# Attention values of head 0 scaled on VectorE instead of ScalarE

## The chip, the core and the metric

The kernel runs on one core of a Trainium2 chip. The metric is device time in microseconds, of which the median of three runs is given. One further execution was taken by the hardware profiler; its times are those of the views below. The engines are TensorE (PE, with its weight loads as PEld), VectorE (DVE), ScalarE (ACT), GpSimd (POOL) and SyncE (SP). [...]

## What is computed

A transformer block in three parts: half a mixture-of-experts layer, attention, and a second half mixture-of-experts layer. Attention has 4 batches of 512 rows with 256 features, and 3 heads. Cut to what matters here:

```
Q = einsum('bne,hde->hbnd', x, Wq); K = ... Wk; V = ... Wv
scores = einsum('hbnd,hbmd->hbnm', Q, K) * scale
w = softmax(scores, axis=2)
attn = einsum('hbnm,hbmd->hbnd', w, V)
out = mean(attn, axis=0) @ fc_w.T + fc_b
```

The softmax runs over axis 2, the query axis `n`, so that the sum that divides belongs to a row `m` of the values. It can therefore be multiplied into the values instead of the scores.

## The kernel before

The block is one long program for one core. The first expert layer, attention for the four batches `b`, and the second expert layer follow each other; the second layer's norm, router and row scatters of a batch are issued inside the attention of the next one. The order of instructions on each engine is made by a scheduler from the program text, the dependencies and some hand-set order constraints; each engine then runs its list in order.

For each batch and head `h`, four steps matter:

- `query(h)` (from L863) multiplies the normed, transposed input `xnT` by the folded weights `A[h]` into the tile `py` (L868). ScalarE copies it to `y` (L872).
- `quadrants(h)` (from L874) forms the 512 x 512 scores in `ex` with seven half-size products (`product(i, ...)`, tile `psc`, L896), as in Strassen's scheme. VectorE combines them (L911, L914, L915, L917, L918, L920), ScalarE copies two (L910, L912) and GpSimd adds one (L913). `exps` then takes the maximum of two slices on VectorE (L903, one reduction over 1024 elements a row) and the exponential on ScalarE (L905), which also yields the sums `z`. L922 makes `rz = 1/z`. `exps(2)` is issued between L918 and L920, `exps(0)` after L920.
- `value(h)` (from L924) computes for each of four slices `m` the product `pv` of `xnT` and `G[h]` (L929; `G` folds the value weights and the output layer), and evicts it from PSUM to `v`, scaled by `rz`. Before the change, head 1 is evicted by VectorE (L934), heads 0 and 2 by ScalarE (L938).
- The loop at the end sums `pa = ex^T v` over heads and slices (L970) and adds it to `x` (L975).

All three heads' scores come first, then all three heads' values. Hence the evictions of head 0 stand next to the score combination and the exponentials of head 2.

PSUM has eight banks here: three in a ring named `mm`, three in a ring named `dn`, and one each for the router's tiles. `py`, `pv`, `pa` and the score products with even numbers use `mm`. The odd-numbered score products use `dn`, as do the transposes `pt_lna` and `pt_ln` of the layernorms (L284). A new tile of a ring can be written once the tile three places earlier has been read out. By the program's text the ring `dn` goes `psc` 7, 5, 3 of head 2, then `pt_lna` (two tiles), then `pt_ln` (two tiles). Product 5 is read by L917 and L918, product 3 by L920.

The transposes belong to the layernorm of the next batch (`lna`) and to that of the second expert layer for the batch before (`ln`). Their results are copied out by ScalarE (L288) and VectorE (L292), and the router's score products `psr` (L335) and rank products `psk` (L400) follow.

Of the kernel before, what the change touches and what calls it, by code (L numbers as in the profile page):

```python
# [21 lines left out]
def tile_macaron_block(  # L22
# [35 lines left out]
    NH = Wq.shape[0]  # L58
# [785 lines left out]
    for b in range(B):  # L844
# [79 lines left out]
        def value(h):  # L924
            v = vs[h] = att.tile([P, NJ, H], F32, tag="y", name=f"v_{b}_{h}", bufs=4)
            for m in range(NJ):
                pv = psum.tile([P, H], F32, tag="mm", name=f"pv_{b}_{h}_{m}")
                for c in range(NC):
                    nc.tensor.matmul(  # L929
                        pv, xnT[:, c, m * P : (m + 1) * P], G[h][:, c, :],  # L930
                        start=(c == 0), stop=(c == NC - 1),
                    )
                if h == 1:
                    nc.vector.tensor_scalar(  # L934
                        v[:, m, :], pv, rzs[h][:, m : m + 1], None, ALU.mult
                    )
                else:
                    nc.scalar.mul(v[:, m, :], pv, rzs[h][:, m : m + 1])  # L938
# [12 lines left out]
        for h in range(NH):  # L951
            value(h)
# [126 lines left out]
```

## Time and profile before

| | us |
|---|---|
| median of 3 runs | 538.14 |
| lowest and highest | 537.95, 538.39 |
| the profiled execution | 540.54 |
| its span | 538.7 |

| group | count | busy us | mean ns |
|---|---|---|---|
| ACT v<-pv,rz (L938) | 32 | 14.7 | 469 |
| DVE v<-pv,rz (L934) | 16 | 7.3 | 480 |
| DVE nmax<-ex (L903), 188 to 400 us | 21 | 25.5 | 1214 |

How to read the views. A row of a timeline gives start and length in us, engine, line, operation, written tile <- read tiles, shapes and the number of merged instructions; in square brackets stands the idle time before it and what ended that. Consecutive starts lie closer together than the lengths, because instructions overlap at their ends. A row of the waits names the waiting engine and line, the line that it waited for, the total in us, how many times, and the longest. Float32 matrix products show as two records for each product.

### The profile page before, as it was taken

The numbers are of one execution on the slowest core, as the hardware profiler recorded it, in microseconds if no ns is written. First come the engines' busy times: TensorE is split into PE (matmuls) and PEld (weight loads), VectorE is DVE, ScalarE is ACT, GpSimd is POOL, SyncE is SP. The second block draws the span as 40 slices with busy tenths as digits, with TensorE's granted clock in tenths as the row PEclk, the third lists the DMA queues.
The fourth block names the chain that finished last, engine by engine and source line by source line (L and its number), as shares of the span: only waits on it lengthen the run. The fifth ranks groups of instructions, "written<-read, shape, count | busy, mean of one in ns | idle before, by whom it ended". The sixth has DMA issues, their size and how long they took to land. (4 is left out here: it accounts for less than half of the span.)

```text
span 538.7 us, 7948 instructions
## 1 busy us (share of the span) xinstructions
PE 484.5 (90%) x2262; PEld 374.9 (70%) x2262; DVE 295.4 (55%) x981; ACT 224.6 (42%) x514; POOL 234.7 (44%) x281
## 2 busy tenths in 40 slices
PE   8977249999999899999999999999999767999984
PEld 4666037888656788678885778867888445788852
DVE  6834345555787771258325883336753642555565
ACT  3743015666543770255402664054630313466630
POOL 2466714665658321242254512553014174355653
PEclk9877769999999999999999999999999886999998
DMA  7993364557420000000012000200002245255856
GB/s 266 357 370 125 118 226 122 164 161 230 170 89 1 2 0 1 0 0 2 2 69 89 0 2 0 79 2 1 1 11 99 64 171 178 90 165 179 273 177 208
DMA packets 34734, 57.39 MB, mean 107 GB/s; under 512 B 4928, under 2 KB 25408, under 8 KB 34688
## 3 DMA queue, kind: packets, MB, share of 16 engines
q1 hardware_dynamic: 25424, 32.99, 19.7%
q0 software_dynamic: 8160, 23.44, 12.0%
q10 hardware_dynamic: 1104, 0.42, 0.3%
q8 instruction: 20, 0.33, 0.3%
q14 instruction: 26, 0.21, 0.1%
HBM read 30.78 MB, written 26.05 MB: 105 GB/s over the span
## 5 line engine op out<-in xcount | busy, mean ns | idle before, releaser
L671 POOL DMA_INDIRECT y_d<-ey,to x82 | 80.0, 976 | 66.5 <-ACT xt L632 45.8
L438 POOL DMA_INDIRECT xn_d<-xn_ln,pos x64 | 62.5, 977 | 91.7 <-DVE fa L489 23.0
L644 PE MATMUL peg<-gu,xt 128*128 x328 | 87.5, 391 | 1.9 <-DVE g L597 1.6
L970 PE MATMUL pa<-v,ex 128*128 128x256 f32 x384 | 86.2, 382 | 0.0
L970 PEld LDWEIGHTS pa<-v,ex 128*128 128x128 f32 x384 | 71.6, 190 | 9.2
L644 PEld LDWEIGHTS peg<-gu,xt 128*128 128x128 f32 x328 | 57.6, 195 | 9.0 <-issue 1.7
L661 DVE COPY hT<-pht 128x128 f32<-128x128 f32 x82 | 23.8, 291 | 60.1 <-issue 28.6
L666 PE MATMUL pey<-dn,hT 128*128 x164 | 50.4, 390 | 5.6 <-DVE hT L661 4.6
L670 ACT ACTIVATE ey<-pey,xg 128x256 f32<-128x256 f32 x82 | 38.9, 474 | 28.0 <-issue 15.7
L929 PE MATMUL pv<-G,xnT_lna 128*128 128x256 f32 x192 | 43.5, 382 | 2.7 <-ACT v L938 2.1
L868 PE MATMUL py<-xnT_lna,A 128*128 128x512 f32 x96 | 42.7, 593 | 1.0 <-DVEq L710 1.0
L929 PEld LDWEIGHTS pv<-G,xnT_lna 128*128 128x128 f32 x192 | 36.0, 190 | 9.6 <-ACT v L938 3.3
L905 ACT ACTIVATE ex<-ex,nmax 128x512 f32<-128x512 f32 x48 | 34.2, 714 | 18.6 <-DVE nmax L903 18.4
L650 ACT ACTIVATE sig<-peg 128x128 f32<-128x128 f32 x82 | 22.8, 278 | 42.7 <-PE peg L644 27.3
L632 ACT COPY xt<-pxt 128x256 f32<-128x256 f32 x82 | 29.8, 366 | 14.6 <-PE pxt L628 8.4
L605 PE MATMUL po<-sd,h 128*128 128x256 f32 x64 | 17.1, 415 | 19.1 <-DVE h L598 17.7
L975 DVE TENSOR_TENSOR x<-x,pa 128x256 f32<-128x256 f32 x16 | 6.7, 420 | 50.1 <-PE pa L970 41.3
L666 PEld LDWEIGHTS pey<-dn,hT 128*128 128x128 f32 x164 | 25.2, 194 | 12.4 <-issue 5.1
L628 PE MATMUL pxt<-ident,xg 128*128 128x128 f32 x164 | 32.3, 279 | 0.9 <-DVE xnT_ln L292 0.8
L872 ACT COPY y<-py 128x512 f32<-128x512 f32 x24 | 13.8, 581 | 46.1 <-PE py L868 46.0
L868 PEld LDWEIGHTS py<-xnT_lna,A 128*128 128x128 f32 x96 | 18.2, 190 | 20.6 <-issue 19.8
L881 POOL TENSOR_TENSOR right<-y 128x256 f32<-128x256 f32 x12 | 9.3, 775 | 50.0 <-ACT y L872 50.0
(201 smaller groups left out, 876.0 us busy)
## 6 DMA issues: line engine op xcount, KB each, us to landing
xg<-xn_d SPq DMA_DIRECT2D x82, 129.0 KB
gu<-ffn_experts_gate_up_dram SPq DMA_DIRECT2D x4, 1024.0 KB
yg<-y_d SPq DMA_DIRECT2D x8, 512.0 KB
y<-y_d SPq DMA_DIRECT2D x6, 512.0 KB
dn<-_L_ffn_experts_down_dram SPq DMA_DIRECT2D x2, 1024.0 KB
x<-in_L_attn_x_dram SPq DMA_DIRECT2D x3, 512.0 KB
out_dram<-x SPq DMA_DIRECT2D x3, 512.0 KB
y_d<-ey,to POOLq DMA_INDIRECT x82
```

What stands on the lines that cost most here:

```text
L438: ins = nc.gpsimd.indirect_dma_start(out=self.xn_v[k * NT + b * NJ + j], out_offset=bass.IndirectOffsetOnAxis(ap=pos[:, k, j : j + 1], axi ...
L628: ins = nc.tensor.transpose(pt[:, c, :], xg[:, c * P : (c + 1) * P], ident)
L632: nc.scalar.copy(xt, pt)
L644: nc.tensor.matmul(pg, xt[:, c, :], gu[:, bass.ds(e, 1), c, :], start=(c == 0), stop=(c == NC - 1),)
L661: self.flips.append(nc.vector.tensor_copy(hT, pt))
L666: self.downed = nc.tensor.matmul(py, hT, dn[:, bass.ds(e, 1), :], start=True, stop=True)
L670: nc.scalar.mul(y, py, xg[:, H + 1 : W])
L671: ins = nc.gpsimd.indirect_dma_start(out=self.y_v[i], out_offset=bass.IndirectOffsetOnAxis(ap=tos[i], axis=0), in_=y, in_offset=None,)
L868: nc.tensor.matmul(py, A[h][:, c, fc * P : (fc + 1) * P], xnT[:, c, :], start=(c == 0), stop=(c == NC - 1),)
L905: nc.scalar.activation(ex[:, m, :], ex[:, m, :], AF.Exp, bias=nmax[:, m : m + 1], accum_out=z[:, m : m + 1],)
L929: nc.tensor.matmul(pv, xnT[:, c, m * P : (m + 1) * P], G[h][:, c, :], start=(c == 0), stop=(c == NC - 1),)
L970: nc.tensor.matmul(pa, es[h][:, m, j * P : (j + 1) * P], vs[h][:, m, :], start=(h == 0 and m == 0), stop=(h == NH - 1 and m == NJ - 1),)
```

## The change

The condition that chooses the engine of an eviction in `value(h)` is widened. `NH` is 3.

```diff
-                if h == 1:
+                if h < NH - 1:
                     nc.vector.tensor_scalar(
                         v[:, m, :], pv, rzs[h][:, m : m + 1], None, ALU.mult
                     )
                 else:
                     nc.scalar.mul(v[:, m, :], pv, rzs[h][:, m : m + 1])
```

The four evictions of head 0 in each batch, 16 in all, are issued on VectorE. Head 1 stays there and head 2 stays on ScalarE. The numbers computed are the same. Since the scheduler places the instructions anew, others move too. On TensorE the transposes (L284), which stood behind all twelve value tiles of a batch, stand after the fourth (batch 0) or the third (batches 1 to 3). In batches 1 and 2 the two halves of `pt_ln` stand on either side of the fourth value tile, and one product of the router's eight is issued before the fifth. ScalarE's copies of the transposed tiles (L288) stand between the two pairs of exponentials of head 2. VectorE's copy (L292) stands ahead of the reciprocal L922 of head 2, and in batches 1 and 2 a second one between the evictions of head 1.

## The prediction

> **What bounds the kernel now.** I read the page's engine shares first, then the waits of TensorE between 186 and 400 us (the four attention batches), then the timelines of TensorE, VectorE and ScalarE around the value products of each batch.
>
> ```profile
> PE 484.5 (90%) x2262; PEld 374.9 (70%) x2262; DVE 295.4 (55%) x981; ACT 224.6 (42%) x514; POOL 234.7 (44%) x281
> L929 PE MATMUL pv<-G,xnT_lna 128*128 128x256 f32 x192 | 43.5, 382 | 2.7 <-ACT v L938 2.1
> ```
>
> TensorE is the busiest engine and the start of the chain that ended last. Its waits in the attention part are short and all but one belong to the value products (L929):
>
> ```profile
> PE pv L929 <- ACT v L938: 2.1, 3, 0.8
> PE py L868 <- DVEq L710: 1.0, 1, 1.0
> PE pv L929 <- DVE ex L915: 0.7, 2, 0.4
> ```
>
> So the most that better placed evictions can win is small, and whatever new wait TensorE gets between 186 and 416 us is paid nearly in full: the only other wait there, at the branch L710, hangs on VectorE's last add of pa (L975), which follows TensorE. Here is batch 1: TensorE, then VectorE, then ScalarE (start, length, engine, line, operation):
>
> ```profile
> 249.40 5.34 PE L929 MATMUL pv<-G,xnT_lna 128*128 128x256 f32 x24
> 255.39 5.45 PE L929 MATMUL pv<-G,xnT_lna 128*128 128x256 f32 x24 [0.65 <-ACT v L938]
> ```
>
> ```profile
> 251.64 0.66 DVE L918 TENSOR_TENSOR ex<-ex,psc 128x512 f32<-128x512 f32 x1
> 252.21 1.21 DVE L903 TENSOR_REDUCE nmax<-ex 128x2 f32<-128x1024 f32 x1
> 253.34 0.68 DVE L920 TENSOR_TENSOR ex<-ex,psc 128x512 f32<-128x512 f32 x1
> 254.05 1.22 DVE L903 TENSOR_REDUCE nmax<-ex 128x2 f32<-128x1024 f32 x1
> 255.19 0.87 DVE L934 TENSOR_SCALAR v<-pv,rz 128x256 f32<-128x256 f32 x2
> ```
>
> ```profile
> 254.18 0.71 ACT L905 ACTIVATE ex<-ex,nmax 128x512 f32<-128x512 f32 x1
> ...
> 254.88 0.45 ACT L938 ACTIVATE v<-pv,rz 128x256 f32<-128x256 f32 x1
> ```
>
> Each value tile is 4 records (192 over 48 tiles). Records start every (5.34 - 0.38) / 23 = 0.216 us, so a tile is 0.863 us. I write V h.m for head h, slice m. All value tiles share three PSUM banks, so each waits for the eviction of the tile three before it: 24 records are six tiles, and the seventh (V1.2) waits for ScalarE to evict the fourth (V0.3). It was due at 249.40 + 24 x 0.216 = 254.58 and came at 255.39: 0.81 us lost, plus 0.10 because the first interval after a stop is 0.32 instead of 0.22. Counted the same way, TensorE loses in the value phases 0.65 us in batch 0 (bank of a score product, L915), 0.91 in batch 1, 0.55 + 1.04 in batch 2, 0.92 in batch 3: 4.1 us in all.
>
> **The change, part by part.** Sixteen evictions (4 in each batch, head 0) leave ScalarE's queue and join VectorE's.
>
> *Cost of one.* L934 takes 478 ns on VectorE and L938 474 ns on ScalarE; three of L934 take 1.28 us, so one every 0.40. [...] The rows show 4 ns, 0.06 us for sixteen. [...]
>
> *Place.* In the built order of the changed program (an order, without times) VectorE's V0.0 stands just behind L920 in batches 1 to 3 (in batch 0 just behind L915), then comes the last L903, and only then V0.1, V0.2, V0.3. Before, ScalarE did V0.0 to V0.2 of batch 1 at 250.95 to 252.66, between two pairs of exps, when it had nothing else to do. The scheduler also moves work on TensorE: the eight transposes of the next layernorm (L284), which came after all value tiles, now stand after V0.3 (batch 0) or V0.2 (the others). They need PSUM banks too: the second of the pair waits for L918, and in batches 1 and 2 the next transposes (pt_ln) wait for L920. No DMA moves; SP's order is unchanged and POOL only swaps one large add (L950) with four small ones, off TensorE's path.
>
> *Batch 1, worked through* (an end of an eviction is seen by TensorE 0.06 us later, as 254.88 + 0.45 to 255.39 shows). V0.0 to V0.2 run from 249.40 to 251.99. The transposes start; the second one waits for L918, 251.64 + 0.66 = 252.30: 0.37 us lost plus restart. Eight of them, 0.109 apart (eight records took 1.04 in all, one 0.272), end at 253.24. pt_ln waits for L920's end, 253.34 + 0.68 = 254.02: 0.84 lost plus 0.10; four end at 254.62. VectorE does V0.0 at 253.94 to 254.42, then L903 at 254.34 (0.29 later than before), then V0.1 at 255.48, V0.2 at 255.88, V0.3 at 256.28. V0.3's product finds its bank free: 254.62 to 255.48. The other half of pt_ln waits for ScalarE's copy of xnT_lna, which can only follow the exps ending at 254.88: ready 255.53, 0.15 lost with restart. One router product waits for the next copy to 256.07. Then V1.0 to V2.3 run, eight tiles without a stop, as V0.1 (255.96), V0.2 and V0.3 are out and V1.0 leaves at about 258.2: to 263.28. The rest of the router products, 14 records 0.1115 apart in the trace, 1.56, end at 264.84. Before, the same work and six records of pa were done at 265.49; those six take 1.30, so 266.14: **+0.65 us**. In short, 0.91 us of old waits go and about 1.6 come.
>
> *Batch 0.*
>
> ```profile
> 190.59 8.94 PE L929 MATMUL pv<-G,xnT_lna 128*128 128x256 f32 x40 [0.38 <-DVE ex L915]
> ```
>
> ```profile
> 190.78 0.68 DVE L917 TENSOR_TENSOR ex<-ex,psc 128x512 f32<-128x512 f32 x1
> 193.17 0.68 DVE L920 TENSOR_TENSOR ex<-ex,psc 128x512 f32<-128x512 f32 x1
> 194.16 1.21 DVE L903 TENSOR_REDUCE nmax<-ex 128x2 f32<-128x1024 f32 x1
> ```
>
> The 0.65 us wait for L915 stays. V0.0 takes the place of a layernorm step on VectorE, L917 comes at 190.95, L920 at 193.28 to 193.96. V0.2 and V0.3 run to 192.43, the transposes to 193.30. Then V1.0 waits for V0.1, which stands behind L920: 193.88 to 194.36, so it starts at 194.42: 1.12 + 0.10 lost. V1.1 waits for V0.2, which stands behind L903 (194.28 + 1.13): it ends at 195.89, so 0.56 + 0.10 lost. Nothing stops after that. pa starts at 202.10 instead of 200.25: **+1.85 us**.
>
> *Batch 2.* As batch 1, with its VectorE steps at 317.49 to 321.7; the old 0.55 for L915 stays, 1.04 goes, and 0.48 + 0.95 + 0.15 + 0.10 come: **+0.65 us**.
>
> *Batch 3.* There is no pt_ln to put between. V0.3 waits for V0.0, behind this L920:
>
> ```profile
> 384.31 0.68 DVE L920 TENSOR_TENSOR ex<-ex,psc 128x512 f32<-128x512 f32 x1
> ```
>
> V0.2 ends at 382.94; 0.38 lost for L918 (383.27); the transposes and two small rank products end at 384.45; V0.0 runs on VectorE at 384.91 to 385.39, so V0.3 starts at 385.45: 1.10 lost with restart. V1.0 waits for V0.1 behind L903, out at 386.92: 0.28. With the small waits for the copy, pa stands where it stood at 395.37 + 0.94 only at 396.5 for the same content: **+1.13 us**.
>
> *Sum.* 1.85 + 0.65 + 0.65 + 1.13 = 4.3 us. The profiled execution had a span of 538.7 and took 540.54, 2.4 above the median of the runs shown (538.14); the sum is a difference taken inside the span (to 543.0) and I add it to the median: **542.4 us**. ScalarE's relief is costed at nothing: its freed 16 x 0.47 = 7.5 us lie where TensorE's progress hides them. If the cover of pulled-up transposes were gone, V0.3 would wait about 2.4 us instead (251.99 to 254.48).
>
> [...]
>
> **Rivals.**
> 1. *The old waits vanish and the pulled transposes cover the new ones: faster.* The three waits for ScalarE, 0.91 + 1.04 + 0.92 = 2.9 us, go: 535.3 us. For it: in batch 1 V0.3's own bank is free in time (254.48 against 254.62). It decides where TensorE reaches the second transposition later than L918 ends, and pt_ln later than L920: in batch 1 it is 0.31 and 0.78 too early (252.0 against 252.30, 253.24 against 254.02). Also against it: VectorE has no gap from 251.64 to 255.19, and V0.1 to V0.3 stand behind a 1.21 us reduction. Chance 0.08.
> 2. *The loss is given back: no change, 538.1.* For it: TensorE has some 29 us of gaps after 410 us, among them 5.45 and 3.46 for POOL's scatters, and 1.16 at the branch. Against it: each of these starts from the last pa add of a batch, so it shifts with TensorE. Chance 0.07.
> 3. *VectorE's lateness spreads* to the softmax sum of head 2 and the router, half a microsecond more in each batch: 544.4. For it: L903 is 0.3 later. Against: head 2's tiles are due some 3 us after the sums. Chance 0.07.
>
> **How the numbers follow.** The forecast, +4.3 (between +2.8 and +5.4), has 0.78. The range 540.0 to 544.0 reaches down to the case that only batch 0's cost is left (+1.9) and up to part of rival 3. This kernel's measurement tells about 0.2% (1.1 us) from no change; slower 0.78 + 0.07 = 0.85, same 0.07, faster 0.08.
>
> **What would show it.** In the new profile: TensorE's waits at L929 <- VectorE v L934 in batch 0 (about 1.1 and 0.6) and batch 3 (about 1.0); waits of L284 for L918 and L920; none for ScalarE L938; pa of batch 0 starting 1.8 us later after the value phase's start. It is wrong if the pulled transposes run without a wait, or if the attention part is longer and the end isn't.

## The result, and the profile after

| | before, us | changed, us |
|---|---|---|
| first comparison: median of 4 executions each | 538.26 | 544.72 |
| lowest and highest | 537.95, 540.02 | 541.9, 546.41 |
| the profiled execution | 540.54 | 541.9 |
| its span | 538.7 | 540.1 |

The ratio is 1.011, with an interval of 1.0067 to 1.0153. The changed kernel is slower, as forecast, by 6.5 us, but 544.72 lies above the top of the predicted range (544.0). Two later comparisons, on the chips numbered 1 and 8, gave 1.0073 (1.0039 to 1.0107) and 1.0077 (1.0048 to 1.0107), medians 3.7 and 3.4 us above the kernel before; they come below. Which chip the first comparison ran on is not on record.

The first part of the page of the changed kernel, and its costliest group in question:

```profile
PE 491.6 (91%) x2261; PEld 377.8 (70%) x2262; DVE 300.7 (56%) x997; ACT 217.3 (40%) x498; POOL 234.6 (43%) x281
L929 PE MATMUL pv<-G,xnT_lna 128*128 128x256 f32 x192 | 44.5, 383 | 3.1 <-DVE v L934 2.3
```

Sixteen more instructions are on VectorE and sixteen fewer on ScalarE, and the releaser of the value tiles has changed from ScalarE's L938 to VectorE's L934. The view of the waits of TensorE over the whole of attention (152.2 to 415.9 us) names them:

```profile
PE pv L929 <- DVE v L934: 2.3, 3, 1.0
PE psc L896 <- ACT y L872: 1.8, 1, 1.8
PE pt_ln L284 <- DVE ex L920: 1.4, 2, 0.7
PE py L868 <- DVEq L710: 1.0, 1, 1.0
PE pv L929 <- DVE ex L915: 0.7, 2, 0.4
PE pt_lna L284 <- DVE ex L918: 0.5, 2, 0.3
PE pt_ln L284 <- DVE ex L918: 0.2, 1, 0.2
```

The 2.1 us for ScalarE are gone. In their place stand 2.3 us for VectorE's evictions and 2.1 us for the score additions L918 and L920, which set the banks of the pulled-up transposes free. Nothing else in the list differs from before: the 1.8 us at the first score products stand in the kernel before too, where attention begins at 155.9 us, and the prediction's view, which began at 186 us, left them out. The list grows by 2.3 us only, because it counts from the end of one record to the start of the next, and these records overlap (they start 0.216 us apart and last 0.38). Counted from start to start, V1.0 in batch 0 waits 1.07 us where the list has 0.91, and the first interval after a stop is longer (0.32 instead of 0.22 us). With eight new waits for three old ones this adds over a microsecond.

The timelines show the waits in place. VectorE in batch 0:

```profile
189.53 0.68 DVE L920 TENSOR_TENSOR ex<-ex,psc 128x512 f32<-128x512 f32 x1
190.12 0.48 DVE L934 TENSOR_SCALAR v<-pv,rz 128x256 f32<-128x256 f32 x1
190.52 1.21 DVE L903 TENSOR_REDUCE nmax<-ex 128x2 f32<-128x1024 f32 x1
191.65 1.26 DVE L934 TENSOR_SCALAR v<-pv,rz 128x256 f32<-128x256 f32 x3
```

and TensorE beside it:

```profile
188.72 1.04 PE L284 MATMUL pt_lna<-ident,xn_lna 128*128 128x128 f32 x8
190.66 1.13 PE L929 MATMUL pv<-G,xnT_lna 128*128 128x256 f32 x4 [0.91 <-DVE v L934]
192.18 6.31 PE L929 MATMUL pv<-G,xnT_lna 128*128 128x256 f32 x28 [0.39 <-DVE v L934]
```

V1.0 starts 0.06 us after V0.1's eviction ends (190.12 + 0.48 = 190.60), V1.1 0.05 after V0.2's (191.65 + 0.48 = 192.13). The reduction L903 lies between the two evictions. In batch 1 the listed waits are both at transposes. A third, too short for the list, follows V0.3: the second half of `pt_ln` starts at 253.57, 0.07 us after its turn and 0.05 after ScalarE's copy L288 has ended:

```profile
250.52 0.96 PE L284 MATMUL pt_lna<-ident,xn_lna 128*128 128x128 f32 x7 [0.18 <-DVE ex L918]
252.15 0.66 PE L284 MATMUL pt_ln<-ident,xn_ln 128*128 128x128 f32 x4 [0.68 <-DVE ex L920]
252.64 1.03 PE L929 MATMUL pv<-G,xnT_lna 128*128 128x256 f32 x4
253.57 0.66 PE L284 MATMUL pt_ln<-ident,xn_ln 128*128 128x128 f32 x4
```

```profile
252.96 0.56 ACT L288 COPY xnT_lna<-pt_lna 128x512 f32<-128x512 f32 x1
```

In batch 3, V0.3 waits for VectorE's eviction of V0.0, which stands behind L920:

```profile
383.36 0.68 DVE L920 TENSOR_TENSOR ex<-ex,psc 128x512 f32<-128x512 f32 x1
383.95 0.48 DVE L934 TENSOR_SCALAR v<-pv,rz 128x256 f32<-128x256 f32 x1
```

```profile
384.49 1.13 PE L929 MATMUL pv<-G,xnT_lna 128*128 128x256 f32 x4 [1.01 <-DVE v L934]
```

**Where the time lies.** I cut each profile at the first record of `py` in batch 0 and the end of the last record of `pa`. The view by stretches gives for each: window, length, busy time of PE, PEld, DVE, ACT and POOL, mean granted TensorE clock, DMA share, GB/s. First the kernel before, then the changed one:

```profile
155.90:415.80 259.90, 254.35 (x1145) 203.48 (x1144) 144.15 (x330) 104.55 (x209) 94.04 (x109) 1.00 0.05 19
0.00:155.90 155.90, 127.09 (x643) 96.01 (x644) 86.85 (x393) 70.93 (x170) 83.24 (x115) 0.89 0.62 205
415.80:538.70 122.90, 103.02 (x478) 75.37 (x476) 64.43 (x259) 49.07 (x135) 57.46 (x57) 0.92 0.52 167
```

```profile
152.20:415.90 263.70, 255.81 (x1144) 203.49 (x1143) 149.84 (x346) 97.28 (x193) 94.39 (x109) 1.00 0.05 19
0.00:152.20 152.20, 129.62 (x642) 97.06 (x644) 86.85 (x393) 71.17 (x170) 82.91 (x115) 0.91 0.65 210
415.90:540.10 124.20, 106.21 (x478) 77.25 (x476) 64.03 (x259) 48.82 (x135) 57.26 (x57) 0.89 0.50 164
```

Attention is 3.85 us longer (259.89 and 263.74 to the record). The two profiled spans differ by 1.4 only, because the first expert layer, whose work and order on the engines the edit doesn't touch, was 3.7 shorter in this execution, and the last layer 1.3 longer. The clock column goes with it: the granted clock is either full or half, in stretches of 3.413 us or multiples of it in the trace's record, so a mean of 0.89 over 155.9 us is 34 us at half speed, and 0.91 over 152.2 is 27. A span of one profiled execution can't size this edit. Its attention part can.

### The profile page after: what moved, and what is told of

It is laid out like the page before. It is cut to its first block, busy times and chain, and to the rows that moved or that the text cites. A ratio compares the mean times of both kernels' runs of the same rounds, so it can differ in the third digit from the quotient of the medians.

```text
span 540.1 us, 7943 instructions
## 1 busy us (share of the span) xinstructions
PE 491.6 (91%) x2261; PEld 377.8 (70%) x2262; DVE 300.7 (56%) x997; ACT 217.3 (40%) x498; POOL 234.6 (43%) x281
## 5 line engine op out<-in xcount | busy, mean ns | idle before, releaser
L644 PE MATMUL peg<-gu,xt 128*128 x328 | 90.1, 400 | 8.4 <-ACT xt L632 5.9
L644 PEld LDWEIGHTS peg<-gu,xt 128*128 128x128 f32 x328 | 59.0, 200 | 16.4 <-ACT xt L632 6.3
L872 ACT COPY y<-py 128x512 f32<-128x512 f32 x24 | 13.7, 580 | 47.1 <-PE py L868 47.1
L628 PEld LDWEIGHTS pxt<-ident,xg 128*128 128x128 f32 x164 | 23.3, 145 | 12.3 <-issue 2.6
```

What stands on the lines that cost most here:

```text
L628: ins = nc.tensor.transpose(pt[:, c, :], xg[:, c * P : (c + 1) * P], ident)
L644: nc.tensor.matmul(pg, xt[:, c, :], gu[:, bass.ds(e, 1), c, :], start=(c == 0), stop=(c == NC - 1),)
```

## The experiments

Each is compared with executions of the kernel before on its own chip. "Attention" is the cut just described.

| run | ratio to before (95% interval) | attention, us | against 259.89 |
|---|---|---|---|
| changed, second time | 1.0073 (1.0039 to 1.0107) | 263.74 | +3.85 |
| batch 0 only | 1.0042 (1.0012 to 1.0072) | 261.68 | +1.79 |
| batches 1 to 3 only | 1.0041 (1.0011 to 1.0071) | 262.01 | +2.12 |
| before, transposes under the wait | 0.9956 (0.9927 to 0.9985) | 257.05 | -2.84 |
| changed, transposes held behind | 1.0272 (1.0236 to 1.0308) | 274.66 | +14.77 |
| before, two rings | 0.9928 (0.9902 to 0.9953) | 255.87 | -4.02 |
| changed, two rings | 0.9984 (0.996 to 1.0009) | 259.72 | -0.17 |
| changed, third time | 1.0077 (1.0048 to 1.0107) | 263.74 | +3.85 |
| before against itself | 0.9996 (0.9972 to 1.0021) | 259.89 | 0.00 |
| two rings, second time | 0.9944 (0.9913 to 0.9974) | 255.87 | -4.02 |
| changed, one more profile | one execution | 263.76 | +3.87 |

**The change again.** No edit.

> The changed kernel once more, in five rounds against the kernel before, to size the effect: the first timing spread from 541.9 to 546.4. Theory A (the whole effect is the new waits of TensorE inside attention): attention takes 263.5 us in the profile again, 3.8 more than before, and the median is 3.5 to 4.5 above the kernel before. Theory B (something outside attention adds about 2 us, such as a lower granted clock in the second expert layer): the median is 5.5 to 7 above, with attention still at 263.5.

Attention was 263.74 again, and the medians were 542.58 (12 executions, 539.61 to 547.19) against 538.89 (35 executions, 535.23 to 542.16), 3.7 apart, as theory A says. The interval, 2.1 to 5.8 us, alone would just reach theory B; that attention accounts for the whole difference is what speaks for A. The spread matters as much: single executions of one kernel range over 7.6 and 6.9 us.

**By batches.** From the kernel before:

```diff
-                if h == 1:
+                if h == 1 or (h == 0 and b == 0):
```

and, in the other run, `b > 0`.

> Only batch 0 evicts head 0 on VectorE. Theory A: attention +1.8 us (waits of 1.07 and 0.55 at the fifth and sixth value tile), median +1.8. Theory B (an effect outside attention that comes with the edit as such): more than +3.

> Only batches 1 to 3 evict head 0 on VectorE. Theory A: +0.5, +0.5 and +1.1 us, together +2.0, and with the batch 0 run it adds up to the whole. Theory B: +4 or so, not additive.

Both kept to theory A: +1.79 and +2.12 add to 3.91, where the whole is 3.85. Each batch has its own cost. In the whole time the medians lie 1.7 and 1.6 us above the kernel before, together 3.35 where the whole edit gave 3.69: beyond the intervals, of about 1.6 us on either side of each, nothing outside attention shows.

**The old wait covered.** From the kernel before, with each value product given its name for the order:

```diff
+        if b > 0:
+            in_turn(f"V1_1_{b}", f"Tlna_{b + 1}" if b + 1 < B else f"Tln1_{b - 1}", f"V1_2_{b}")
         for j in range(NJ):
             pa = psum.tile([P, H], F32, tag="mm", name=f"pa_{b}_{j}")
```

> The engines of the kernel before (head 0 on ScalarE), but in batches 1 to 3 the transposes of the next layernorm are ordered between the sixth and the seventh value tile, where TensorE waited 0.8 to 0.9 us for ScalarE. Theory A (TensorE sets the pace, and a wait covered by work that must be done anyway is won): three waits of about 0.9 us vanish, attention -2.6, median -2.6 (535.7). Rival: the transposes' own PSUM banks or copies make new waits, as they did in the changed kernel, and the time stays within 1 us of the kernel before.

Attention fell by 2.84 us, and the waits of its TensorE in attention (154.7 to 411.7 us) were:

```profile
PE psc L896 <- ACT y L872: 1.8, 1, 1.8
PE py L868 <- DVEq L710: 1.0, 1, 1.0
PE pv L929 <- DVE ex L915: 0.7, 2, 0.4
```

The three waits for ScalarE are gone and the transposes made none. In batches 1 to 3 of the changed kernel the same eight transposes stand 3 tiles earlier, where banks of the score products were still being read. So here work that had to be done anyway hid a wait where its own inputs and banks were ready, and made new waits where they were not: three for L918, 0.7 us in all.

**The cover taken away from the changed kernel.** From the changed kernel, again with the value products named:

```diff
+        in_turn(f"V2_3_{b}", f"Tlna_{b + 1}" if b + 1 < B else f"Tln1_{b - 1}")
+        if 0 < b < B - 1:
+            in_turn(f"V2_3_{b}", f"Tln1_{b - 1}")
```

> The changed kernel (heads 0 and 1 on VectorE), with the transposes held behind all twelve value tiles as in the kernel before. Theory A (VectorE's late evictions hold the three banks, and the pulled-up transposes hide part of it): batch 1 waits 2.6 for V0.0 and 0.7 for V0.1, batches 2 and 3 alike, batch 0 loses 2.1 and 0.7 at V1.0 and V1.1; attention +9.5 us against the kernel before, about +5.7 against the changed one. Rival (the pulled-up transposes are themselves the harm, since they wait for L918 and L920): attention falls back towards the kernel before, under +3.

The rival is out: the pulled-up transposes are a help and not the harm. In attention TensorE's order is that of the kernel before again, but for two small rank products of batch 3, and the late evictions alone cost more than the whole edit did. The first wait of each batch came about as worked out: 1.94, 2.48, 2.60 and 2.41 us from start to start, where 2.1 and three times 2.6 were expected. The second wait came in batches 0 and 1 (0.55 each, 0.7 expected), and not in batches 2 and 3. The list has six waits for eight expected:

```profile
PE pv L929 <- DVE v L934: 9.6, 6, 2.4
```

Even so the whole was +14.8 and not +9.5. I put the missing 5 us down to the clock. Two stretches of its TensorE show it, one just after a wait in batch 0 and one in batch 1:

```profile
176.80:179.90 3.10, 3.10 (x9) 2.44 (x9) 1.61 (x5) 0.74 (x3) 0.00 (x0) 0.52 0.00 0
241.40:245.00 3.60, 3.60 (x11) 2.85 (x10) 1.18 (x4) 0.57 (x2) 0.00 (x0) 0.55 0.00 0
```

The last column but two is the granted clock: about half. Records start 0.427 us apart there, instead of 0.216. Each batch has one such stretch of 3.413 us in the trace's clock record, 13.7 us in all. At that pace half the records are done in it, so up to 1.7 us are lost in each, 6.8 at most (an estimate from these spacings). The second waits of batches 2 and 3, 1.4 us as expected, did not come because TensorE ran at half speed there and reached those tiles later; 6.8 - 1.4 = 5.4. In the changed kernel itself, the waits at value tiles and transposes reach 1.16 us at most and the clock stays at 1.00.

**More banks.** In the kernel before, and then in the changed one:

```diff
-                pv = psum.tile([P, H], F32, tag="mm", name=f"pv_{b}_{h}_{m}")
+                pv = psum.tile(
+                    [P, H], F32, tag="dn" if NJ * h + m in (2, 6, 7) else "mm", name=f"pv_{b}_{h}_{m}"
+                )
```

> The engines of the kernel before, but value tiles 2, 6 and 7 of each batch's twelve take banks of the ring dn, so that they find banks of score products that are read out early, and no tile waits for V0.3 or L915. Theory A (the three banks of one ring are what turns a late eviction into a wait): all 4.1 us of waits at value tiles vanish, attention 255.8, median -4 (about -0.75%). Rival (the waits are the evicting engines' pace, not the banks): they reappear at the next tiles or at the transposes, and the gain stays under 1.5.

> The same banks with the engines of the changed kernel. Theory A: V1.0 still waits for V0.0 behind L920 (0.8 with restart) in batches 1 to 3 and batch 0 loses about 0.8, in all 3.4 against 4.1 in the kernel before: attention 259.3, within 1 us of the kernel before and 4.5 under the changed one, but 3.4 above the same banks with head 0 on ScalarE. Rival (VectorE lacks the time, so that more banks don't help): attention stays at 263 or more.

With head 0 on ScalarE all twelve tiles of batch 1 run in one piece, 48 records in 10.52 us; with 47 intervals of 0.216 and one record of 0.38 they need 10.53:

```profile
229.50 10.52 PE L931 MATMUL pv<-G,xnT_lna 128*128 128x256 f32 x48
```

All 4.0 us of waits at value tiles are gone. The order of TensorE, VectorE and ScalarE in attention is that of the kernel before, instruction for instruction, so only the banks differ there. With head 0 on VectorE, on the same banks, one wait is left in that batch:

```profile
229.80 4.48 PE L931 MATMUL pv<-G,xnT_lna 128*128 128x256 f32 x20
234.87 6.31 PE L931 MATMUL pv<-G,xnT_lna 128*128 128x256 f32 x28 [0.59 <-DVE v L936]
```

L936 is the eviction L934 of this file. On the new ring scheme the edit costs 259.72 - 255.87 = 3.85 us in attention. That the old scheme gave the same sum is chance: by batch it is 0.61, 0.86, 1.52 and 0.86 us here and 1.79, 0.49, 0.49 and 1.08 there. The expectation of 3.4 was too low, most of all in batch 2. TensorE's order is the same in both two-ring versions, but for four transposes of batch 0, so here the late evictions cost what they cost without the moved transposes. In the whole time the two-ring versions lie 0.56% apart (0.9984 and 0.9928), about 2.9 us. So in these versions the banks set how long TensorE went on beside a late eviction, and the edit makes the evictions late; the extra banks buy back about as much (4.02 us in attention) as the edit costs (3.85). The rival for each run fails. What no run tried is to place the evictions of head 0 earlier in VectorE's list, ahead of a reduction. How much of the 3.85 us lies in the engine's load and how much in this order is open.

**Again, with a control.** The changed kernel, the kernel before and the two-ring version were run side by side on another chip, with one more profile of the changed one. No edits.

> The changed kernel a third time. Theory A (the effect is the 3.85 us in attention, and what lay beyond it in the first timing is scatter of the two expert layers, which the edit leaves alone): attention 263.7 us once more, ratio 1.007 (+3.5 to +4.5). Theory B (the edit costs about 6 us, the rest in a lower TensorE clock in some executions): ratio 1.010 or more, or an attention part above 265 in a profile.

> The kernel before against itself, to see what a timing of nothing gives. Theory A: attention 259.9 in its profile, ratio within 0.3% of 1, single executions spread over 5 us or more. Theory B: its executions agree within 2 us, so that a median of four can't be 2 off by chance.

> The version with value tiles 2, 6 and 7 in the other ring, once more beside the other two. Both theories: attention 255.9, ratio 0.992 to 0.993.

> One more profile of the changed kernel. Theory A: attention 263.7 again; the first expert layer and the last may differ by 2 us and more from the earlier profiles of the same chip. Theory B: in some profile the attention part shows half-speed records of TensorE and is longer.

Attention came out at 263.74, 259.89, 255.87 and 263.76. The ratio of the changed kernel was 1.0077, medians 514.38 against 510.95; its interval too just reaches theory B's 1.010, and no profile of it has attention above 265. The control gave 0.9996, but with an interval of 0.25% either side, from 12 and 24 executions spread over 508.96 to 512.8 and 507.89 to 514.08, 3.8 and 6.2 us: nearer to theory A's spread than to B's. The two profiles of the changed kernel on this chip did not show the scatter that theory A allowed for the layers: the first layer took 136.1 and 137.2 us, the last 111.0 and 110.8. The two-ring version gave 0.9944 (medians 507.57 against 510.95), a little less gain than expected, but its interval (0.9913 to 0.9974) takes in the expected ratio. It has the shortest attention of all versions.

## Why the prediction was right or wrong

| term of the sum | predicted, us | measured in attention, us |
|---|---|---|
| batch 0 | +1.85 | +1.79 |
| batch 1 | +0.65 | +0.49 |
| batch 2 | +0.65 | +0.49 |
| batch 3 | +1.13 | +1.08 |
| sum | +4.3 | +3.85 |

The measured terms are the times from one batch's first `py` record to the next one's, and for batch 3 to the end of `pa`. The mechanism held at nearly every place. Right were: the wait for L915 in batch 0 that stays; V1.0 behind V0.1 and V1.1 behind V0.2 there (1.12 and 0.56 predicted, 1.07 and 0.55 in the trace, start to start); in batches 1 and 2 the transposes waiting for L918 and L920 (0.84 predicted for L920, 0.84 measured) and V0.3 finding its bank free; V0.3 and V1.0 behind VectorE in batch 3 (1.00 and 0.18 predicted without restarts, 1.16 and 0.24 measured).

In batches 1 and 2 the sum was 0.16 too high in each. The short wait for ScalarE's first copy came (0.12 with its restart, 0.15 predicted), the one charged before the router's product did not, and the restarts at the transposes took 0.03 to 0.06 instead of 0.10. That the eviction takes VectorE as long as ScalarE held too: 476 ns median for 32 instructions, 474 for ScalarE's 16. Back to back they differ a little more: in the kernel before, the closest pairs start 0.36 us apart on ScalarE and 0.39 on VectorE, 0.5 us for sixteen and small beside the 3.85. No run shows the terms behind the bounds +2.8 and +5.4 of the forecast; the runs showed these 0.03 us for each eviction, and +3.85 in attention. The loss was not given back: the branch L710 still cost TensorE 1.0, and the later comparisons found 3.7 and 3.4 us of the 3.85 in the whole time.

What failed is the step from the sum to the time: "the sum is a difference taken inside the span (to 543.0) and I add it to the median: **542.4 us**", with the range made from the bounds of that sum alone, "down to the case that only batch 0's cost is left (+1.9) and up to part of rival 3". The scatter of the rest of the kernel was put at next to nothing: "This kernel's measurement tells about 0.2% (1.1 us) from no change". I took three executions within 0.44 us of each other for the kernel's spread, although the profiled one lay 2.4 above their median. The runs showed that the expert layers, which the edit leaves alone, carry several microseconds of scatter from one execution to the next: on one chip 35 executions of the kernel before ranged from 535.23 to 542.16, and six profiles there and in the first comparison had a first layer of 152.0 to 155.9 us and a last one of 122.1 to 126.1. The first comparison's 544.72 was a median of four, with an interval of 2.3 us on either side of its ratio; a range for it needed about that much more at both ends. Against a median of twelve the 542.4 was near (542.58), but partly by luck: the kernel before lay 0.75 above the 538.14 that the sum was added to, and the difference was 3.7 and not 4.3.

That the first comparison's surplus over 3.85 us lay in those layers is inferred. Of its four executions of the changed kernel only the fastest has a profile here, and that one shows attention at 263.74. The three other profiles of the changed kernel, on chips 1 and 8, show the same to 0.02 us, and no half-speed stretch in attention. The granted clock of each execution points the same way. It gives the time at half speed: 43 to 66 us in the 35 executions of the kernel before on chip 1, whose time rises by 0.25 us with each microsecond of it (correlation 0.83). The four executions of the first comparison had 59.7 us of it on average, the twelve of the second 54.7. By that slope about 1.2 us of the 1.8 between their means go with the clock, which is an estimate. Where in the three executions without a profile the half speed lay is not on record, and a surplus of a microsecond or two that belongs to that comparison alone isn't excluded by the ratios, whose intervals overlap.

Of the rivals, the first (old waits vanish, pulled transposes cover the new ones) had its idea right and its place wrong: the covered version shows that it wins 2.8 us where the banks are free. The estimate in the prediction that V0.3 "would wait about 2.4 us instead" without the cover (2.49 by its own figures) was right for the wait (2.4 to 2.6 in batches 1 to 3) and missed the half-speed stretch of 3.413 us that each batch had with such a wait.

## What to carry to other kernels

Moving these evictions was no gain, though one takes as long on VectorE (476 ns) as on ScalarE (474): VectorE worked back to back just there (251.64 to 255.19 us in batch 1 of the kernel before), and attention took 3.85 us more. So ask what stands in the engine's queue ahead of the eviction, and which product waits for the bank. With the ring of three banks, two remedies won time in the kernel before: early-needed tiles on banks whose readers finish early (4.02 us of attention), and independent work under the wait at a point where its own banks are ready (2.84 us). And size an edit of about one per cent by the part of the trace that it touches; give the prediction of a whole time the scatter of the parts that it doesn't touch, here 6.9 us between the lowest and the highest of 35 executions.

## What the runs showed of the hardware

With the transposes held behind, the waits of TensorE cost more than their length: attention took 14.77 us more, where 9.5 had been worked out from the waits alone. Each batch had a wait of 1.9 to 2.6 us, in batches 0 and 1 with a second of 0.55 soon after it, and each was followed by a stretch of 3.413 us at a granted clock of half. In attention of the other versions, waits up to 1.2 us were not, and neither was the single one of 1.8 at the first score products. By my count of idle time on the grid of the clock record, the stretches that were followed by half speed had 1.86 to 2.28 us idle of 3.41, and all others in the attention parts of thirteen profiles at most 1.80. All four half-speed stretches in attention come from one profile of one kernel, and no run set the idle time on purpose, so these counts give no limit. In the first expert layer of the kernel before, 3.41 us with only 1.01 idle (9.58 to 12.99 us) came right before a half-speed stretch.

The chips differ: the kernel before took 538.9 us on chip 1 and 510.4 and 511.0 on chips 6 and 8 (538.3 in the first comparison). Its attention was the same to 0.01 us in the first comparison and on chip 8, the two places where it was profiled. The first expert layer took 152 to 156 us in the profiles of the first comparison and of chip 1, and 136 to 137 in those of chips 6 and 8.
